# A four-layer convolution chain: eighteen blocks ahead of the projection in layer 0, and waves in pairs in the tail

## The chip, the cores and the metric

The kernel runs on one core of one Trainium2 chip. The metric is the device time of one execution in microseconds (us); what counts is the median over several runs. The core has a matrix engine (TensorE, PE in the profile, with its weight loads as a row of their own, PEld), a vector engine (VectorE, DVE), an engine for activation functions (ScalarE, ACT), a general engine (GpSimd, POOL) and one that here issues the transfers (SyncE, SP). Matmuls write to PSUM, which has eight banks of 128 x 512 float32; DVE and ACT take the results from there to SBUF.

## The reference

The input x is 4 images of 16 channels, 512 x 512, float32. Four layers follow each other.

```python
# layer 0: a window transformer block (windows of 8 x 8, 2 heads of 8, 64 hidden)
x = x + depthwise3x3(x) + pos_b
q, k, v = qkv(affine1(window(x)))
out = softmax(q * 8 ** -0.5 @ k.T) @ v
x = x + (out @ proj_w.T + proj_b)
x = x + gelu(affine2(x) @ fc1_w.T + fc1_b) @ fc2_w.T + fc2_b
# layer 1: fake-quantised 3x3 convolution, batch norm, clip
y = conv(quant(x), quant(weight))
x = clip((y - mean(y)) / sqrt(var(y) + eps) * gamma + beta, 0, 6)
# layer 2: two 3x3 convolutions and a residual
x = conv(relu(conv(x, w1) + b1), w2) + b2 + x
# layer 3: 3x3 convolution, 16 -> 128 -> 16 per pixel, a residual
x = x + (relu(conv(x, conv_w) * w1 + b1) * w2 + b2)
```

The statistics of layer 1 need all of layer 0, and the values of layers 1 to 3 need the statistics. So there are three stretches: layer 0, a pass for the statistics, and a tail that computes layers 1 to 3 together.

## The kernel before

**Layer 0** (`window_attention`) does 64 steps; in each it works on 4 strips pairs by 4 images of a window row. The order of the instructions on every engine is the program's, written out by hand (a manual schedule). A step `n` has two halves. The first runs over eight parts of windows: `scores` (L348) and `values` (L333) on TensorE, the exponential on ACT (L356), `attend` (L369), and on DVE and POOL `divide` (L384, L389, L391) and `turn_back` (L398), which puts the normalised result into `o`. The second half mixes work of three steps on TensorE:

- blocks `q`: queries of step n+1 (L314), emptied to `g` by ACT (L319) in the first part and by DVE (L321) later;
- blocks `d`: one tap of the depthwise convolution of step n+2 for one image (L287), summed in PSUM banks 0 to 3;
- `project` (L404): reads `o`, writes banks 6, 7, 4, 5 in two rounds (one for each head), and DVE adds the result to `y`, one bank at a time (L409);
- blocks `h`: a hidden part of the two-layer perceptron of step n (L416), which reads `y`, each followed by a Gelu on ACT (L421).

One block is four matmuls on one quarter of TensorE's rows; which quarter is given by the block's index modulo 4. Blocks `q` and `h` take PSUM banks 4 to 7 in turn, so each waits until the former user of its bank has been emptied. A string of letters gives the order. Sixteen blocks stand ahead of `project`, 44 behind it:

```python
        for i, what in enumerate("qqddddqqqqdddddd"):
            block(what, i, bank(next(free)) if what == "q" else None, True)
        if more:
            highest(n + 1)
        y = ys.pop(n)
        project(y)
```

Behind the second half come the first `values` and `scores` of the next step, and `output` (L427, L434), which reads the hidden parts.

**The statistics** are a short stretch of bfloat16 convolutions, which the change does not touch.

**The tail** (`conv_layers`) is a software pipeline over 128 tiles of four image rows. In step `T` each stage works on another tile: `load(T + 3)` from HBM (L940), `quantised(T + 2)` (DVE L1010, ACT L1013), and on TensorE `stage_z(T)`, layer 1's convolution in bfloat16; `stage_h(T - 1)` and `stage_x(T - 3)`, layer 2; `stage_y(T - 4)`, layer 3's convolution; four waves `wave(T - 6, k)` (L1197), which widen `y` to 128 channels; and `outputs(T - 7)` (L1217), which narrows them again. All four convolutions are matmuls of the same shape, 64 rows by 32 columns, of L1122, eight side by side. A wave is four matmuls of 32 rows by 128 columns side by side, each to a bank of its own. The output has 128 rows by 32 columns. DVE and ACT share the emptying: L1205 and L1207 for the waves, L1181 and L1182 for `y`, L1170 for `x` (DVE alone), L1159 and L1160 for `h`, L1141, L1142 for `z` and, on DVE, L1143, which caps `z` at 0 and 6; L1223 for the output.

PSUM's eight banks go round: `take(n)` gives the next n, whoever asks. A stage that asks waits until the bank's former user has been emptied. A step takes 26 banks: two for each convolution and the output, four for each wave.

Between stages a tile is also copied to a second buffer shifted by two rows (`shift`, `shift_ends`: L1064, L1067), four transfers each for `qo`, `xo`, `ho` and `zo`. SP issues them and the loads and the store (L1226) one after the other in the program's order. `stage_y(T - 4)` reads `xo`, which `stage_x` of the step before made.

The order on TensorE in the tail is that of the calls in the loop: outputs, wave, y, wave, x, wave, h, z, wave.

Of the kernel before, what the change touches and what calls it, by code (L numbers as in the profile page):

```python
# [29 lines left out]
TP = H // 4  # L30
NH, HD = 2, 8
WS = 8
T = WS * WS
# [110 lines left out]
def window_attention(ctx: ExitStack, tc, xw, x1, hots, m, v, peak):  # L144
# [138 lines left out]
    def depthwise(n, tap, u):  # L283

        dy, dx = divmod(tap, 3)
        for vv in range(V):
            nc.tensor.matmul(  # L287
                bank(u)[quad(vv)], taps[quad(u), tap, :],
                xts[n][quad(u), vv, dy : dy + WS, dx : dx + BW],
                start=tap == 0, stop=tap == 8,  # L290
            )

    def position(n, i):

        if n not in ys:
            ys[n] = px.tile([P, U, N], F32, tag="y", name=f"y{n}", bufs=3)
        for u in (2 * i, 2 * i + 1):
            nc.vector.tensor_scalar(  # L298
                by_window(ys[n][:, u]), by_row(bank(u)), v("pos_b"), None, ALU.add
            )  # L300
# [11 lines left out]
    def query(y, h, vv, b, scalar=False):  # L312
        for u in range(U):
            nc.tensor.matmul(  # L314
                b[quad(u)], wg[h][quad(vv)], y[quad(vv), u, :], start=True, stop=True
            )
        out, src = g[:, vv, :, h, :], b.rearrange("p (j t) -> p j t", t=T)
        if scalar:
            nc.scalar.activation(out, src, AF.Identity, bias=gb[:, h : h + 1])  # L319
        else:  # L320
            nc.vector.tensor_scalar(out, src, gb[:, h : h + 1], None, ALU.add)  # L321
# [6 lines left out]
    def values(k):  # L328

        vv, jl = k // 2, 4 * (k % 2)  # L330
        b, t = bank(4 + 2 * (k % 2)), yts[k % 3]
        for jj in range(4):
            nc.tensor.transpose(  # L333
                b[:, P * jj : P * jj + P],
                y2[:, vv, jl + jj].rearrange("p w t -> p (w t)"), m("ident"),
            )
        src = b.rearrange("p (a w c) -> p a w c", w=2, c=C)
        if 0 < k < 7:
            nc.scalar.copy(t[:, :, 0:3:2], src)
        else:  # L340
            nc.vector.tensor_copy(t[:, :, 0:3:2], src)
# [20 lines left out]
    def attend(e, k):  # L362

        t = yts[k % 3]
        for jj in range(4):
            for u in range(U):
                for w in range(2):
                    half = slice(64 * w, 64 * w + 64)
                    nc.tensor.matmul(  # L369
                        bank(4 + 2 * (k % 2) + w)[quad(u), P * jj : P * jj + P],  # L370
                        t[half, U * jj + u, w : w + 2].rearrange("p d c -> p (d c)"),
                        e[half, u, jj, :],
                        start=True, stop=True,
                    )
# [129 lines left out]
    for n in range(STEPS):  # L504
        more, ahead = n + 1 < STEPS, n + 2 < STEPS
        taken, asked = [0] * U, [0] * V

        def block(what, i, b, scalar=False):
            at = i % 4
            if what == "q" and more:  # L510
                query(ys[n + 1], asked[at], at, b, scalar)
                asked[at] += 1
            elif what == "d" and ahead:
                depthwise(n + 2, taken[at], at)
                taken[at] += 1
                if at % 2 and taken[at - 1 : at + 1] == [9, 9]:
                    position(n + 2, at // 2)

        values(0)
        es, ts = {0: scores(0, n)}, {}  # L520
        if last:

            output(*last)
        for k in range(1, 8):
            es[k] = scores(k, n)
            values(k)
            attend(es[k - 1], k - 1)
            ts[k - 1] = divide(k - 1, n, nc.gpsimd)
            if 1 < k < 7:
                turn_back(ts[k - 2], k - 2)  # L530
            if k == 1:
                send(8 * U)
            if k % 2 and more:
                turn_keys(ys[n + 1], k // 2)
            if k < 5:
                highest_output()
        nc.scalar.preload_act_table_set("gelu_and_others")
        attend(es[7], 7)
        ts[7] = divide(7, n, nc.gpsimd)
        for k in (5, 6, 7):  # L540
            turn_back(ts[k], k)
        free = iter((4, 5, 6, 7, 4, 5))
        for i, what in enumerate("qqddddqqqqdddddd"):
            block(what, i, bank(next(free)) if what == "q" else None, True)
        if more:
            highest(n + 1)
        y = ys.pop(n)
        project(y)
        if n % 2 == 0:
            xo = px.tile([P, U, WS, XW], F32, tag="xo", name=f"xo{n}", bufs=1)  # L550
        if not more:
            flag = bounded()

        hids, units, sent = [[] for _ in range(U)], itertools.cycle((6, 7, 4, 5)), 0
        used = [0] * U
        for i, what in enumerate("ddddhdhddhqqhddhdhddhdhddhddhddhdhddddhhddhh"):
            if what == "h":
                at = i % 4  # L560
                u = used[at]
                used[at] += 1
                if not more and sent < u and len(hids[sent]) == U:
                    output(y, xo, hids[sent], (sent,), (sent,), n)
                    send(8, queues)
                    sent += 1
                hids[u].append(hidden(y, u, at, bank(next(units)), n))
            else:
                block(what, i, bank(next(units)) if what == "q" else None)
        if n + 4 < STEPS:  # L570
            xts[n + 4] = load(n + 4)
        if more:
            nc.scalar.preload_act_table_set("natural_log_exp_and_others")
        last = (y, xo, sum(hids, []), range(U), (5, 4, 6, 7), n)
# [372 lines left out]
def conv_layers(ctx: ExitStack, tc, x1, out, cw, cq, sw, m, v, peak):  # L947
# [29 lines left out]
    ze, zo, he, ho = ring("ze", 4), ring("zo", 3), ring("he", 2), ring("ho", 2)  # L977
# [19 lines left out]
    def inner(t):  # L997
        return t[:, :, 1 : W + 1]
# [137 lines left out]
    def stage_z(n):  # L1136

        if not 0 <= n < TP:
            return
        p, z = convolve(cq, ((qe(n), 0), (qo(n), 1))), inner(ze(n))  # L1140
        nc.scalar.activation(z[:, 0], p[0], AF.Identity, bias=shift_by, scale=scale)  # L1141
        nc.vector.tensor_scalar(z[:, 1], p[1], scale, shift_by, ALU.mult, ALU.add)  # L1142
        nc.vector.tensor_scalar(z, z, ACT_MAX, 0.0, ALU.min, ALU.max)  # L1143
        shift_ends(n, ze, zo)

# [42 lines left out]
    def wave(n, k):  # L1188

        if not 0 <= n < TP:  # L1190
            return []
        units, p = [], take(4)
        for q in range(4):
            w, f = divmod((k + q) % 4, 2)
            par = w ^ (q % 2)
            src = ye(n + (w and not q % 2))
            nc.tensor.matmul(  # L1197
                p[q], w1[_quad(q), 1 - par, :], inner(src)[_quad(q), f, :],
                start=True, stop=True,
            )  # L1200
        for q in range(4):
            w, f = divmod((k + q) % 4, 2)
            hd = ld.tile([P, W], F32, tag="hid", name=f"hid{n}_{k}_{q}", bufs=24)
            if next(count) % 2:
                nc.scalar.activation(hd, p[q], AF.Relu, bias=v("l3_b1"))  # L1205
            else:
                nc.vector.tensor_scalar(hd, p[q], v("l3_b1"), 0.0, ALU.add, ALU.max)  # L1207
            units.append((q // 2, 2 * f + w, w ^ (q % 2), hd))
        return units

    def outputs(n, units):

        if not units:
            return
        p, o, seen = take(2), inner(xe(n)), set()
        for r, c, par, hd in units:
            nc.tensor.matmul(  # L1217
                p[r][_quad(c)], w2[:, par], hd,
                start=(r, c) not in seen, stop=(r, c) in seen,
            )  # L1220
            seen.add((r, c))
        for r in range(2):
            nc.vector.scalar_tensor_tensor(  # L1223
                o[:, r], p[r], v("l3_b2"), o[:, r], ALU.add, ALU.add
            )
        nc.sync.dma_start(out[n], o)  # L1226

    units = []
    for T in range(TP + 7):
        if T + 3 <= TP:  # L1230
            load(T + 3)
        outputs(T - 7, units)
        units = wave(T - 6, 0)
        stage_y(T - 4)
        units += wave(T - 6, 1)
        if T + 2 <= TP:
            quantised(T + 2)
        stage_x(T - 3)
        units += wave(T - 6, 2)
        stage_h(T - 1)  # L1240
        stage_z(T)
        units += wave(T - 6, 3)


def _strips(a):
# [127 lines left out]
```

## Time and profile before

| what | value |
|---|---|
| median of 3 runs | 5648.19 us (5645.71 to 5648.49) |
| profiled execution | 5653.74 us |
| its span | 5651.9 us |
| granted TensorE clock, mean | 0.990 |
| TensorE matmul busy | 5441.0 us (96%) |
| DVE busy | 3826.3 us (68%) |
| ACT busy | 3427.9 us (61%) |
| L287 matmuls (taps) | 18432 records, 603 ns each |
| L404, L409 | projection, and DVE's adds behind it |
| L1197 matmuls (waves) | 4096 records, 639 ns each |
| L1217 matmuls (outputs) | 4096 records, 595 ns each |
| L1207, DVE, one wave part | 1024 of 512 columns, 744 ns each |
| L1205, ACT, one wave part | 1024 of 512 columns, 685 ns each |
| `xo<-xe` transfers | 512 of 128.5 KB, 2.4 us from issue to landing |

The profile is of one execution. Its slices cut the span into 40 equal parts; a digit is the busy share in tenths. A timeline has the start of an instruction (or of several alike that follow each other), how long it took, engine, line, operation, and the tiles it writes and reads; in brackets how long the engine was idle before it, and what ended that. "x8" are eight records: a float32 matmul is two passes and has two. Records of matmuls that run side by side on different parts of the array overlap, so their durations do not add up; the distance between starts does. "issue" as the end of an idle time means that the profile shows no wait.

### The profile page before, as it was taken

The page shows a single profiled execution, that of the slowest core. Times are in us where ns is not written, and L with a number is a line of the kernel's source. Part 1 is how long each engine was busy: PE and PEld are TensorE (multiplying, and loading weights), DVE is VectorE, ACT ScalarE, POOL GpSimd, SP SyncE. Part 2 cuts the span into 40 slices and gives each one's busy share as a digit, 9 for nine tenths or more (in the row PEclk, how much of TensorE's full clock was granted, in tenths as well). Part 3 has the DMA queues.
Part 4 walks back from the last instruction along what each step waited for, and adds up shares of the span by engine and source line. Part 5 has one row for each costly group of instructions (what it writes and reads, how often), then busy time and mean ns, then how long its engine had stood idle before and what let it go on. Part 6 is the DMA issues. An engine that isn't in the chain of part 4 may idle for free. (4 is left out here: it accounts for less than half of the span.)

```text
span 5651.9 us, 268227 instructions
## 1 busy us (share of the span) xinstructions
PE 5441.0 (96%) x120912; PEld 2960.7 (52%) x120912; DVE 3826.3 (68%) x5934; ACT 3427.9 (61%) x4610; POOL 707.4 (13%) x692
## 2 busy tenths in 40 slices
PE   7999999999999999999999666999999999999999
PEld 5777777767677777777776332222222222222222
DVE  4667666666667766666666454667677676777676
ACT  3777777777777777777777453444444444444444
POOL 1111111111111111111111452000000000000000
PEclk9999999999999999999999898999999999999999
DMA  2333333332333333333332797767777767777774
GB/s 79 78 76 77 77 74 80 73 80 66 77 72 82 73 82 73 80 73 80 74 79 41 167 246 178 174 174 178 173 178 173 177 173 176 175 175 175 175 177 107
DMA packets 626192, 677.45 MB, mean 120 GB/s; under 512 B 355856, under 2 KB 485008, under 8 KB 616848
## 3 DMA queue, kind: packets, MB, share of 16 engines
q1 hardware_dynamic: 624240, 658.76, 48.6%
q8 instruction: 953, 15.61, 1.2%
q14 instruction: 199, 1.63, 0.1%
q0 software_dynamic: 512, 1.05, 0.1%
q10 hardware_dynamic: 288, 0.39, 0.0%
HBM read 222.45 MB, written 134.48 MB: 63 GB/s over the span
## 5 line engine op out<-in xcount | busy, mean ns | idle before, releaser
L356 ACT ACTIVATE e<-pair 128x1024 f32<-128x1024 f32 x1024 | 993.0, 1022 | 488.8 <-PE pair L348 488.1
L287 PE MATMUL pair<-x,taps 32*32 32x512 f32 x18432 | 1043.2, 603 | 4.2 <-issue 2.4
L1205 ACT ACTIVATE hid<-tb,vec 128x512 f32<-128x512 f32 x1024 | 647.8, 685 | 630.4 <-PE tb L1197 630.4
L384 DVE STREAM_TRANSPOSE a<-bank 128x512 f32<-128x512 f32 x1024 | 669.7, 692 | 320.2 <-PE bank L369 298.6
L391 POOL TENSOR_TENSOR t<-a,r 128x512 f32<-128x512 f32 x512 | 542.0, 1059 | 2561.3 <-DVE r L389 2561.3
L421 ACT ACTIVATE hid<-bank,f1b 128x512 f32<-128x512 f32 x1024 | 653.5, 687 | 332.7 <-PE bank L416 245.7
L348 PE MATMUL pair<-g,y 32*128 32x128 f32 x16384 | 757.7, 286 | 3.7 <-issue 2.0
L1207 DVE TENSOR_SCALAR hid<-tb,vec 128x512 f32<-128x512 f32 x1024 | 718.2, 744 | 27.1 <-PE tb L1197 26.8
L348 PEld LDWEIGHTS pair<-g,y 32*128 32x128 f32 x16384 | 650.5, 186 | 153.5 <-issue 136.6
L416 PE MATMUL bank<-y,fc_e 32*32 32x512 f32 x8192 | 722.3, 610 | 0.6 <-DVE y L409 0.4
L369 PE MATMUL bank<-e,yt 64*32 64x128 f32 x32768 | 604.1, 274 | 22.4 <-ACT e L356 12.8
L287 PEld LDWEIGHTS pair<-x,taps 32*32 32x32 f32 x18432 | 531.3, 103 | 164.6 <-issue 54.8
L1197 PE MATMUL tb<-ye,mat 32*128 32x512 f32 x4096 | 586.1, 639 | 0.0
L369 PEld LDWEIGHTS bank<-e,yt 64*32 64x32 f32 x32768 | 459.6, 106 | 122.1 <-issue 92.1
L1217 PE MATMUL tb<-hid,mat 128*32 128x512 f32 x4096 | 466.0, 595 | 0.0
L298 DVE TENSOR_SCALAR y<-pair,vec 128x512 f32<-128x512 f32 x256 | 180.3, 747 | 349.8 <-PE pair L287 349.8
L1122 PE MATMUL tb<-zo,cw 64*32 64x512 f32 x3096 | 365.7, 598 | 16.2 <-issue 8.9
L1122 PE MATMUL tb<-xo,cw 64*32 64x512 f32 x3096 | 360.5, 592 | 5.9 <-ACT hid L1205 2.1
L1122 PE MATMUL tb<-ho,cw 64*32 64x512 f32 x3072 | 358.4, 592 | 3.7 <-issue 3.2
L1197 PEld LDWEIGHTS tb<-ye,mat 32*128 32x128 f32 x4096 | 162.8, 183 | 377.5 <-issue 370.4
L1122 PE MATMUL tb<-ze,cw 64*32 64x512 f32 x3072 | 359.9, 598 | 0.0
L1122 PE MATMUL tb<-he,cw 64*32 64x512 f32 x3072 | 358.1, 592 | 0.0
(178 smaller groups left out, 7111.1 us busy)
## 6 DMA issues: line engine op xcount, KB each, us to landing
x<-in_xw_dram SPq DMA_DIRECT2D x64, 1320.0 KB, 5.7
zo<-ze SPq DMA_DIRECT2D x512, 128.5 KB, 2.4
ho<-he SPq DMA_DIRECT2D x512, 128.5 KB, 2.4
xo<-xe SPq DMA_DIRECT2D x512, 128.5 KB, 2.4
y<-y SPq DMA_DIRECT2D x2048, 32.0 KB, 2.7
tx<-x SPq DMA_DIRECT2D x256, 256.0 KB, 4.0
out_dram<-xe SPq DMA_DIRECT2D x128, 512.0 KB, 4.6
x<-xo SPq DMA_DIRECT2D x1008, 64.0 KB, 2.8
```

What stands on the lines that cost most here:

```text
L287: nc.tensor.matmul(bank(u)[quad(vv)], taps[quad(u), tap, :], xts[n][quad(u), vv, dy : dy + WS, dx : dx + BW], start=tap == 0, stop=tap == 8,)
L348: nc.tensor.matmul(bank(u)[:, P * jj : P * jj + P], y2[quad(u), vv, jl + jj].rearrange("p w t -> p (w t)"), g[quad(u), vv, jl + jj].rearra ...
L356: nc.scalar.activation(e[:, 2 * i : 2 * i + 2].rearrange("p u j t -> p u (j t)"), pairs[i], AF.Exp,)
L369: nc.tensor.matmul(bank(4 + 2 * (k % 2) + w)[quad(u), P * jj : P * jj + P], t[half, U * jj + u, w : w + 2].rearrange("p d c -> p (d c)"), ...
L384: nc.vector.transpose(a[:, 512 * w : 512 * w + 512], bank(4 + 2 * (k % 2) + w))
L391: engine.tensor_tensor(t.rearrange("p b w c -> p w b c"), top, r.unsqueeze(3).to_broadcast([P, 2, 16, C]), ALU.mult,)
L416: nc.tensor.matmul(b[quad(k)], fc1[quad(vv), quad(k)], y[quad(vv), u, :], start=True, stop=True,)
L421: nc.scalar.activation(hd, b, AF.Gelu, bias=f1b)
L1122: nc.tensor.matmul(p[r][_quad(2 * f + w)], weights[_half(r), odd, dx, :], src[_half(r), f, dx : dx + W], start=dx == 0, stop=dx == 2,)
L1197: nc.tensor.matmul(p[q], w1[_quad(q), 1 - par, :], inner(src)[_quad(q), f, :], start=True, stop=True,)
L1205: nc.scalar.activation(hd, p[q], AF.Relu, bias=v("l3_b1"))
L1207: nc.vector.tensor_scalar(hd, p[q], v("l3_b1"), 0.0, ALU.add, ALU.max)
```

## The change

In layer 0 two `d` blocks are taken out behind the projection and put ahead of it. The index behind it now starts at 2, so each remaining block keeps its quarter of rows as far as its place in the string is unchanged; among the first ten the quarters of single blocks differ, and the first three hidden blocks are of quarters 2, 0, 1 in place of 0, 2, 1.

In the tail the four waves of a step stand in two pairs: both of the first pair behind `stage_y`, both of the second behind `stage_z`. The capping of `z` and its shift are a function of their own, `capped`, called behind the second pair. `outputs` stands at the end of a step and takes the waves of the same step, so the loop has one pass fewer. On TensorE the order becomes y, wave, wave, x, h, z, wave, wave, outputs. On SP the store now stands ahead of the next step's load.

```diff
         free = iter((4, 5, 6, 7, 4, 5))
-        for i, what in enumerate("qqddddqqqqdddddd"):
+        for i, what in enumerate("qqddddqqqqdddddddd"):
             block(what, i, bank(next(free)) if what == "q" else None, True)
...
-        for i, what in enumerate("ddddhdhddhqqhddhdhddhdhddhddhddhdhddddhhddhh"):
+        for i, what in enumerate("ddddhdhhqqhddhdhddhdhddhddhddhdhddddhhddhh", 2):
...
         nc.vector.tensor_scalar(z[:, 1], p[1], scale, shift_by, ALU.mult, ALU.add)
+
+    def capped(n):
+
+        if not 0 <= n < TP:
+            return
+        z = inner(ze(n))
         nc.vector.tensor_scalar(z, z, ACT_MAX, 0.0, ALU.min, ALU.max)
         shift_ends(n, ze, zo)
...
-    units = []
-    for T in range(TP + 7):
+    for T in range(TP + 6):
         if T + 3 <= TP:
             load(T + 3)
-        outputs(T - 7, units)
-        units = wave(T - 6, 0)
         stage_y(T - 4)
-        units += wave(T - 6, 1)
+        units = wave(T - 6, 0) + wave(T - 6, 1)
         if T + 2 <= TP:
             quantised(T + 2)
         stage_x(T - 3)
-        units += wave(T - 6, 2)
         stage_h(T - 1)
         stage_z(T)
-        units += wave(T - 6, 3)
+        units += wave(T - 6, 2) + wave(T - 6, 3)
+        capped(T)
+        outputs(T - 6, units)
```

## The prediction

> **What bounds the kernel now.** I read the page first: the slices, then the chain. TensorE is busy at a full granted clock almost everywhere, and the chain that ended last lies wholly on TensorE lines of the tail (the slices from the 25th on). So a microsecond counts only if TensorE gets it.
>
> ```profile
> PE   7999999999999999999999666999999999999999
> ...
> PEclk9999999999999999999999898999999999999999
> ...
> PE 38%; SPq 0%; DMA 0%; ACT 0%; issue 0%; DVE 0%; DVEq 0%
> ```
>
> A busy TensorE is not one without gaps, so I went on to the timeline of one tail step. Steps are exact repeats: of the 128 distances between first `y` matmuls, 121 are 16.71 to 16.72 us.
>
> ```profile
> 4503.03 1.14 PE L1197 MATMUL tb<-ye,mat 32*128 32x512 f32 x8
> 4503.19 0.59 ACT L1181 COPY ye<-tb 128x512 f32<-128x512 f32 x1 [1.44 <-PE tb L1122]
> 4503.30 0.69 DVE L1182 COPY ye<-tb 128x512 f32<-128x512 f32 x1 [1.20 <-PE tb L1122]
> ...
> 4510.51 0.40 PE L1122 MATMUL tb<-qe,cq 64*32 64x512 bf16 x4
> ...
> 4511.30 1.14 PE L1197 MATMUL tb<-ye,mat 32*128 32x512 f32 x8
> ...
> 4511.58 0.80 DVE L1142 TENSOR_SCALAR ze<-tb,scale,shift 128x512 f32<-128x512 f32 x1
> ...
> 4512.37 3.64 PE L1217 MATMUL tb<-hid,mat 128*32 128x512 f32 x32
> ```
>
> The reader is to see pitches, not durations. In the same timeline weight loads of a float32 convolution come four to a tile row every 0.43 us; that is one pass. A convolution of `y`, `x` or `h` is 6 passes (2.58), a wave 2 (0.86), an output 8 (3.44), the bfloat16 `z` three half passes (0.64). One step is 3 x 2.58 + 4 x 0.86 + 3.44 + 0.64 = 15.26. The other 1.45 us sits where the tile shape changes: a wave takes 1.07 to the next start (4511.30 to 4512.37), 0.21 more than its passes; going into a wave costs 0.13 to 0.16 (`y` 4500.30 to 4503.03 is 2.73); `h` to `z`, both 64*32, costs 0.02.
>
> In layer 0 I read the stretch in which queries, taps, projection and hidden layer follow each other, 18.7 us of a step of about 47.8.
>
> ```profile
> 2014.49 3.67 ACT L319 ACTIVATE g<-bank,gb 128x512 f32<-128x512 f32 x6 [0.97 <-PE bank L314]
> ...
> 2017.60 0.60 PE L287 MATMUL pair<-x,taps 32*32 32x512 f32 x2
> 2017.64 2.29 PE L404 MATMUL bank<-o,wo 32*32 32x512 f32 x50
> ...
> 2019.78 2.73 DVE L409 SCALAR_TENSOR_TENSOR y<-bank,pb,y 128x512 f32<-128x512 f32 x4 [0.34 <-issue]
> ...
> 2021.72 2.13 ACT L421 ACTIVATE hid<-bank,f1b 128x512 f32<-128x512 f32 x3 [3.56 <-PE bank L416]
> ```
>
> These lines come from the answers by engine, put in order of time. The projection (L404) starts in the very stretch in which the last taps (L287) start: there is no hole in front of it to fill. What follows hangs on it: the adds (L409) at a pitch of 0.66, the first hidden block after the first add, the Gelus.
>
> **Part 1, layer 0: two tap blocks ahead of the projection.** Nothing is added or removed; in 62 of the 64 steps two blocks of taps, on rows 0 to 31 and 32 to 63, go from behind the projection to its front. Each is 4 matmuls of 2 passes on one row quarter, so 0.86 us of that quarter. No DMA, DVE or POOL work moves, and ACT's order stays but for which hidden block comes first.
>
> What they leave is idle time: behind the projection TensorE waits for the adds. Hidden blocks start 0.05 us or so after an add frees their bank (medians: add ends 3.23 and 3.88, hidden 3.32 and 3.94 after the projection's start). The later sixth-and-seventh hidden blocks wait for DVE to empty the second query (7.80, then 7.85). So two blocks fewer there bring nothing forward, and all of it moves with the first add.
>
> What they cost: 16 blocks stand from 2013.36 to about 2017.60, 0.265 each, so two make 0.53. By rows it is more: row quarter 0 has the new block, then its projection, and the first add needs that quarter alone, +0.86. There is one slack: the fourth bank of the projection waits for ACT's sixth query (ends 2018.16), and the first add never comes sooner than 1.30 us after that end; the median of 61 steps is 1.43, the step shown 1.62. So 0.1 to 0.3 of the delay may hide behind ACT in some steps. In the step without any taps in front (the last but one) the first add comes 6.02 us after the first query, at the median 6.53: the taps already stick out. Ends 0.3 and 0.86; I take 0.55, nearest to the row of 16 blocks. Sum 62 x 0.55 = **+34 us** (19 to 53).
>
> **Part 2, tail: two double waves.** Order now: y w x w h z w o w. After: y ww x h z ww o. Shape changes fall from eight to five: into a wave twice (0.16, 0.13), out twice (0.21), and `o` to `y`, which the trace does not have. Its bounds: 0.13 (`o` to wave: 3.57 - 3.44) and 0.21; out of a 32-column shape every row shows 0.13 to 0.16, so 0.13.
>
> The Trainium skill speaks for it and against it on one page, TensorEngine Tiling (Array Packing). Its Key Properties say that a change of tiling mode drains TensorE. At this step's own 1.45/8 = 0.18 a change, three fewer would save 0.54 us, 121 x 0.54 = 65 us. Its section on the PSUM bottleneck says that tiling speeds the matmuls up and not the emptying of PSUM, which may become the limit. This decides here: the eight banks go round, and the second wave of each pair takes the banks of the last two stages, its last two those of the convolution just before it. The trace has that case once, at the end, where `h` and `z` have run out:
>
> ```profile
> 5608.71 2.75 PE L1197 MATMUL tb<-ye,mat 32*128 32x512 f32 x16
> 5608.87 1.41 DVE L1170 SCALAR_TENSOR_TENSOR xe<-tb,vec,ze 128x512 f32<-128x512 f32 x2 [1.40 <-PE tb L1122]
> ...
> 5610.33 0.29 PEld L1197 LDWEIGHTS tb<-ye,mat 32*128 32x128 f32 x2 [0.36 <-DVE xe L1170]
> 5611.39 3.64 PE L1217 MATMUL tb<-hid,mat 128*32 128x512 f32 x32
> ```
>
> The last two matmuls of the pair start at 5610.33, 0.05 after DVE's second eviction, and the next stage 1.06 later. I use both figures.
> - Behind `y`: DVE's copy ends 0.96 after the pair's start (4503.30 + 0.69 - 4503.03), the second wave wants the bank at 0.86: +0.15. The pair takes 0.96 + 0.05 + 1.06 = 2.07.
> - Behind `z`: DVE's part ends 1.87 after `z` starts (4512.38 - 4510.51), so the output starts at 1.87 + 0.05 + 1.06 = 2.98 after `z`, 0.28 later than free banks would allow.
> - Sum from `y` to `y`: 2.73 + 2.07 + 2.60 (`x`) + 2.60 (`h`) + 2.98 + 3.57 = 16.55, against 16.71: -0.16.
>
> The cap of `z` goes behind the four DVE units of the pair. It would end 5.3 us after `z` starts; its transfers stand on SP behind those of `h` and do not need it sooner (before, SP issued them 5.3 to 7.4 after `z`), and `h` reads them one step later. The store moves ahead of the next load on SP; the load is used a step later. Both cost nothing under this cover; a late `zo` would hold `h`.
>
> The quantising moves on its engines: DVE does four units, not two, before `L1010`, so `qe` is ready 1.32 later (four units at 0.66) relative to `y`, and with it SP's four `qo` and four `xo` transfers. The last `xo` lands 14.80 (median; 15.65 at the latest of 80 steps) after `y` starts, so then 16.12 (16.97), and the next `y` wants it at 16.55. About one step in five waits, up to 0.4: +0.04 on the mean. So -0.12 a step, 121 x 0.12 = **-14 us** (-19 to -4). In the last steps without `x` four waves stand together where three did: +2. One pass of the loop fewer saves nothing; the same matmuls run.
>
> **Sum.** +34 - 14 + 2 = +22 on the profiled execution's 5653.74 (span 5651.9). That execution lies 5.5 above the median of the runs, 5648.19; moved onto the median: **5670 us**.
>
> **Rivals.**
> - *ACT hides the taps.* If the first add hangs on ACT's sixth query in most steps, the two blocks cost nothing: 5648 - 12 = 5636. For it: the correlation of the add with that query's end, 0.78. Against: 0.13 to 0.32 us lie between them already. Faster by 0.2%, on the other side.
> - *The waves pay in full.* If the banks come free in time, the skill's 65 us count: 5648 + 34 - 65 = 5617. Against: the stall at 5610.33.
> - *The transfers decide.* If `xo` lands 0.5 later on average than I move it, every `y` waits about 0.4 more, from the point where landing passes 16.55: 121 x 0.3 = +36 in place of -14: 5648 + 34 + 36 + 2 = 5720. For it: SP issues back to back from `qo` to the store.
> - *The taps move nothing* because the planner restores the order: excluded, the program's order shows them in front.
>
> **Chances.** My forecast 0.60, ACT hides 0.19, full pay 0.08, transfers 0.13. No change means within 11 us, about what a measurement here can tell. The forecast's own range is 5650 to 5697 and reaches into no change with a small part. Slower 0.64, same 0.16, faster 0.20. The range for 8 in 10: 5630 to 5703.
>
> **What would show it.** Right: the first L409 add 0.4 to 0.9 later after the first query, layer 0 steps near 48.4; tail steps 16.5 to 16.65, weight loads of the second wave released by DVE `ye` and `ze`. Wrong: the add unmoved (ACT hides), steps near 16.2 (full pay), or `y` waiting for `xo` in most steps.

## The result, and the profile after

| | before | after |
|---|---|---|
| median of 4 runs each | 5646.95 us (5642.49 to 5648.49) | 5702.02 us (5687.94 to 5703.92) |
| ratio, 95% interval | | 1.0096 (1.0076 to 1.0117) |
| profiled execution, its span | 5653.74, 5651.9 us | 5700.55, 5698.7 us |
| granted clock, mean | 0.990 | 0.992 |
| layer 0: start to the first matmul of the last projection | 3118.3 us | 3176.2 us |
| from there to the first `y` matmul | 385.5 us | 383.0 us |
| tail: first `y` matmul to the end | 2148.1 us | 2139.6 us |
| one step of layer 0, mean of steps 3 to 60 | 47.83 us | 48.86 us |
| one steady tail step, mean of 121 | 16.715 us | 16.605 us |

The kernel became slower by 55 us where +22 was forecast. The three stretches of the profiled executions add up to the spans' difference: +57.8 - 2.5 - 8.5 = +46.8. So all of the loss is in layer 0, and the tail gained.

First the page of after: two rows of slices, and the Gelu group (partitions x elements, count | busy us, ns of one | idle us of ACT ahead of the group, and what ended most of it).

```profile
PE   7999999999999999999999765999999999999999
...
PEclk9999999999999999999999998999999999999999
...
L421 ACT ACTIVATE hid<-bank,f1b 128x512 f32<-128x512 f32 x1024 | 638.6, 686 | 402.2 <-PE bank L416 378.8
```

The same group on the page of before:

```profile
L421 ACT ACTIVATE hid<-bank,f1b 128x512 f32<-128x512 f32 x1024 | 653.5, 687 | 332.7 <-PE bank L416 245.7
```

Slices and clock read as before: they cannot show a per cent. The Gelu group can. It does the same 1024 activations at the same 686 ns, but ACT's idle time ahead of them grew by 69.5 us, and it ends with TensorE's hidden matmuls (L416). Something in front of the hidden layer is late.

The timeline of one layer 0 step of after, with the lines of three engines put in order of time, shows where:

```profile
2058.00 0.66 PE L314 MATMUL bank<-y,wg 32*32 32x512 f32 x8
...
2059.13 3.67 ACT L319 ACTIVATE g<-bank,gb 128x512 f32<-128x512 f32 x6 [1.19 <-PE bank L314]
...
2062.68 0.61 PE L404 MATMUL bank<-o,wo 32*32 32x512 f32 x1
...
2065.39 2.73 DVE L409 SCALAR_TENSOR_TENSOR y<-bank,pb,y 128x512 f32<-128x512 f32 x4 [1.39 <-issue]
...
2067.64 1.84 ACT L421 ACTIVATE hid<-bank,f1b 128x512 f32<-128x512 f32 x3 [4.85 <-PE bank L416]
```

Counted from the first query (2058.00; in the step shown of before 2013.36), the first add stands at 7.39 where it stood at 6.42, and the first Gelu at 9.64 where it stood at 8.36. ACT's queries are no later (2059.13 is 1.13 after the first query, as 2014.49 was). The distance from the add to the Gelu grew as well, from 1.94 to 2.25, although nothing there was touched but the order of the hidden blocks. Means over the steps, in us from the first query:

| | before | after |
|---|---|---|
| first projection matmul | 4.20 | 5.02 |
| end of ACT's sixth query | 5.21 | 5.13 |
| first add | 6.67 | 7.38 |
| first hidden matmul | 7.55 | 8.49 |
| first Gelu | 8.69 | 9.78 |
| last Gelu's end | 20.35 | 21.25 |
| the whole step | 47.83 | 48.86 |

The waits of ACT between 1000 and 3000 us say it once more (us in total, times, longest). Before:

```profile
ACT hid L421 <- PE bank L416: 147.5, 129, 3.9
ACT hid L421 <- DVE y L409: 51.8, 15, 3.8
```

After:

```profile
ACT hid L421 <- PE bank L416: 241.2, 155, 5.1
...
ACT hid L421 <- DVE y L409: 4.0, 1, 4.0
```

Per step that is 199.3 / 41.8 = 4.8 us before and 245.2 / 40.9 = 6.0 after.

The timeline of one tail step of after, TensorE with two lines of DVE (wave lines are L1203 now, outputs L1223):

```profile
4588.55 2.14 PE L1203 MATMUL tb<-ye,mat 32*128 32x512 f32 x16
...
4588.82 0.69 DVE L1188 COPY ye<-tb 128x512 f32<-128x512 f32 x1 [1.45 <-PE tb L1122]
...
4590.61 0.63 PE L1122 MATMUL tb<-he,cw 64*32 64x512 f32 x4
...
4595.79 0.39 PE L1122 MATMUL tb<-qe,cq 64*32 64x512 bf16 x4
...
4596.60 2.24 PE L1203 MATMUL tb<-ye,mat 32*128 32x512 f32 x16
...
4596.86 0.80 DVE L1142 TENSOR_SCALAR ze<-tb,scale,shift 128x512 f32<-128x512 f32 x1
...
4597.53 0.47 PEld L1203 LDWEIGHTS tb<-ye,mat 32*128 32x128 f32 x6 [0.20 <-ACT ze L1141]
...
4598.77 3.64 PE L1223 MATMUL tb<-hid,mat 128*32 128x512 f32 x32
...
4602.34 0.63 PE L1122 MATMUL tb<-xo,cw 64*32 64x512 f32 x4
```

The pair behind `y` takes 4590.61 - 4588.55 = 2.06, the output starts 4598.77 - 4595.79 = 2.98 after `z`, and the output takes 4602.34 - 4598.77 = 3.57 to the next `y`. Weight loads of the second pair wait for the eviction of `z` (4597.53). In the pair behind `y` the profile records no such wait. But of its second wave's four matmuls the last, which writes the bank that DVE empties, starts at 4589.56, 0.05 after DVE's copy ends (4588.82 + 0.69), and its second pass comes at 4590.10, where the other three have theirs at 4589.95. The step from 4585.81 to 4602.34 is 16.53.

### The profile page after: what moved, and what is told of

It is laid out like the page before. It is cut to its first block, busy times and chain, and to the rows that moved or that the text cites. A ratio compares the mean times of both kernels' runs of the same rounds, so it can differ in the third digit from the quotient of the medians.

```text
span 5698.7 us, 268595 instructions
## 1 busy us (share of the span) xinstructions
PE 5485.7 (96%) x120912; PEld 3116.7 (55%) x120912; DVE 3826.3 (67%) x5934; ACT 3386.4 (59%) x4610; POOL 707.5 (12%) x692
## 5 line engine op out<-in xcount | busy, mean ns | idle before, releaser
L287 PE MATMUL pair<-x,taps 32*32 32x512 f32 x18432 | 1022.3, 601 | 2.9 <-DVE y L298 1.5
L421 ACT ACTIVATE hid<-bank,f1b 128x512 f32<-128x512 f32 x1024 | 638.6, 686 | 402.2 <-PE bank L416 378.8
L1213 DVE TENSOR_SCALAR hid<-tb,vec 128x512 f32<-128x512 f32 x1024 | 697.7, 745 | 39.8 <-PE tb L1203 27.3
L416 PE MATMUL bank<-y,fc_e 32*32 32x512 f32 x8192 | 696.2, 600 | 0.8 <-DVE y L409 0.6
L1211 ACT ACTIVATE hid<-tb,vec 128x512 f32<-128x512 f32 x1024 | 619.6, 688 | 112.1 <-PE tb L1203 111.8
L287 PEld LDWEIGHTS pair<-x,taps 32*32 32x32 f32 x18432 | 504.1, 103 | 186.1 <-issue 66.1
L1203 PE MATMUL tb<-ye,mat 32*128 32x512 f32 x4096 | 564.6, 622 | 0.0
L1187 ACT COPY ye<-tb 128x512 f32<-128x512 f32 x129 | 75.7, 587 | 659.5 <-PE tb L1122 659.5
L1223 PE MATMUL tb<-hid,mat 128*32 128x512 f32 x4096 | 466.0, 595 | 0.0
L1203 PEld LDWEIGHTS tb<-ye,mat 32*128 32x128 f32 x4096 | 256.1, 183 | 261.6 <-issue 219.7
```

Of the source, the lines that this page charges most:

```text
L287: nc.tensor.matmul(bank(u)[quad(vv)], taps[quad(u), tap, :], xts[n][quad(u), vv, dy : dy + WS, dx : dx + BW], start=tap == 0, stop=tap == 8,)
L416: nc.tensor.matmul(b[quad(k)], fc1[quad(vv), quad(k)], y[quad(vv), u, :], start=True, stop=True,)
L421: nc.scalar.activation(hd, b, AF.Gelu, bias=f1b)
L1203: nc.tensor.matmul(p[q], w1[_quad(q), 1 - par, :], inner(src)[_quad(q), f, :], start=True, stop=True,)
L1223: nc.tensor.matmul(p[r][_quad(c)], w2[:, par], hd, start=(r, c) not in seen, stop=(r, c) in seen,)
```

## The experiments

Each run was timed against the kernel before on the same chip. Layer 0 of the five kernels that have the order of before there differs between profiles (steps of 47.78, 47.83, 47.94, 48.00 and 48.01 us, mean 47.91), so a difference of 0.2 in a step means little alone. The changed kernel's step is 1.03 over before's own profile and 0.95 over that mean. Steadier is the stretch inside a step from the first add to the last Gelu's end: 13.67 or 13.68 us in all five. Such marks are read beside the step. Tails are compared by their own steps.

### The two halves of the change apart

`l0_alone` is the kernel before with the two strings of layer 0 from the change:

```
-        for i, what in enumerate("qqddddqqqqdddddd"):
+        for i, what in enumerate("qqddddqqqqdddddddd"):
...
-        for i, what in enumerate("ddddhdhddhqqhddhdhddhdhddhddhddhdhddddhhddhh"):
+        for i, what in enumerate("ddddhdhhqqhddhdhddhdhddhddhddhdhddddhhddhh", 2):
```

> Layer 0 as changed, the tail as before. The changed kernel's layer 0 took 47.83 to 48.86 us a step, some 58 us over all its steps. If the two parts do not touch each other, this run is 55 to 62 us over before. If the two parts share something (the same loads, the clock), it differs from 58 by more than 10.

`tail_alone` is the changed kernel with the two strings of before.

> The tail as changed, layer 0 as before. By the sum of the tail (16.72 to 16.61 a step over 121 steps, 4 to 5 us more at both ends): 7 to 12 us under before. If the double waves paid what three changes of shape cost, it would be 65 under; if they only cost, it is over before.

| | median, before beside it | ratio (95%) | layer 0 step | tail step |
|---|---|---|---|---|
| `l0_alone` | 5710.02, 5645.74 | 1.0109 (1.0091 to 1.0126) | 48.92 | 16.715 |
| `tail_alone` | 5632.5, 5645.74 | 0.9976 (0.9966 to 0.9985) | 47.78 | 16.612 |

The halves do not touch each other: their ratios multiply to 1.0085, inside the interval of the whole, and each has the step lengths of the changed kernel. Layer 0 costs about 64 us alone (51 to 71 by the interval, 55 to 62 expected), the tail brings 13 (9 to 19, 7 to 12 expected).

### Which quarters the two blocks load

The blocks of the change lie on row quarters 0 and 1. Both of these kernels keep the order of the hidden blocks of before (quarters 0, 2, 1) and take two blocks to the front, on quarters 0 and 1 or on 2 and 3. `rows_0_1`:

```
-        for i, what in enumerate("qqddddqqqqdddddd"):
+        for i, what in [*enumerate("qqddddqqqqdddddd"), (0, "d"), (1, "d")]:
...
         for i, what in enumerate("ddddhdhddhqqhddhdhddhdhddhddhddhdhddddhhddhh"):
+            if i in (0, 1):
+                continue
```

> Two tap blocks ahead of the projection as in the change, on row quarters 0 and 1, but the order behind it is that of before with these two left out, so the hidden blocks keep their quarters 0, 2, 1. Theory of the row quarter (a new block holds up the projection of its own quarter, 0.86 us, and the first add needs quarter 0): first add +0.7 to +0.86 a step, 43 to 55 us. Theory of the queue (each block ahead costs 0.265 us of TensorE wherever it is): +0.53, 33 us. Theory of ACT (the add hangs on ACT's last query): 0. What this run is under the run of layer 0 alone is the price of the order of the hidden blocks.

`rows_2_3` has 2 and 3 in place of 0 and 1 in both places.

> The same with the two blocks on row quarters 2 and 3. Theory of the row quarter: quarters 2 and 3 are needed by the third and fourth add, 1.3 and 2.0 us after the first, so the first add moves only as far as the in-order issue of the projection's fourth part holds up its fifth: 0.1 to 0.5 a step, 6 to 31 us, and clearly less than on quarters 0 and 1. Theory of the queue: the same 33 us as on quarters 0 and 1. Theory of ACT: 0.

| us from the first query | before | `rows_0_1` | `rows_2_3` | `l0_alone` |
|---|---|---|---|---|
| first projection matmul | 4.20 | 5.04 | 4.87 | 5.02 |
| first add | 6.67 | 7.43 | 7.31 | 7.39 |
| first hidden matmul | 7.55 | 8.24 | 8.11 | 8.49 |
| first Gelu | 8.69 | 9.37 | 9.24 | 9.79 |
| step | 47.83 | 48.57 | 48.37 | 48.92 |

`rows_0_1` took 5682.48 against 5645.74, ratio 1.006 (1.0036 to 1.0083); `rows_2_3` 5671.59, 1.0056 (1.0039 to 1.0072).

Three things follow. First, with blocks on quarters 2 and 3, quarter 0, which the first add needs, has no new work, and still its projection starts 0.67 later and the add 0.64, where 0.1 to 0.5 was expected if only the row quarter counted. The projection stands behind the two blocks in TensorE's order and pays for them wherever they lie. Second, on quarters 0 and 1 the projection starts 0.84 later, near the quarter's 0.86, and the add 0.76: lying on the add's own quarter costs 0.17 more at the projection and 0.12 at the add. Over the mean of five, the step is 0.66 longer on quarters 0 and 1, and 0.46 on 2 and 3. By time the two cannot be told apart: 37 us (20 to 47) and 26 us (22 to 41) over before, with 33 expected from the queue in both, and 43 to 55 and 6 to 31 from the row quarter. So the queue counts, and ACT, from which 0 was expected in both, does not. That the quarter adds to it is likely, but small beside the noise: the five kernels of one order differ by up to 0.13 at the projection and 0.09 at the add. Third, `rows_0_1` has the same adds as `l0_alone` to 0.04, and its hidden matmuls 0.25 and its Gelus 0.42 earlier. These two differ only behind the projection: `rows_0_1` has two taps and then the hidden block of quarter 0, `l0_alone` four taps and then that of quarter 2.

From the timeline of `rows_2_3`, the first four blocks of a step, its adds and its first Gelus:

```profile
2036.48 0.66 PE L314 MATMUL bank<-y,wg 32*32 32x512 f32 x8
2036.53 0.69 PE L287 MATMUL pair<-x,taps 32*32 32x512 f32 x8
...
2043.70 2.73 DVE L409 SCALAR_TENSOR_TENSOR y<-bank,pb,y 128x512 f32<-128x512 f32 x4 [1.22 <-issue]
...
2045.63 2.00 ACT L421 ACTIVATE hid<-bank,f1b 128x512 f32<-128x512 f32 x3 [4.09 <-PE bank L416]
```

From add to Gelu it is 1.93, as before (1.94), not 2.25. The first two lines show that the forecast's 0.265 is the mean of a full queue and not the price of a place in it: two query blocks and two taps, on four different quarters, all start here within 0.13 us. Once every quarter has work, a block can start only when its own quarter is free, and the program's order keeps what stands behind it waiting; that this is how blocks on quarters 2 and 3 hold up quarter 0 is read from the order, not shown by a run of its own.

### The order of the hidden blocks alone

`hidden_2_first` leaves the front of before as it is and only lets the hidden block of quarter 2 come ahead of that of quarter 0, as the change does:

```
-        for i, what in enumerate("ddddhdhddhqqhddhdhddhdhddhddhddhdhddddhhddhh"):
+        for i, what in [
+            (0, "d"), (1, "d"), (2, "d"), (3, "d"), (2, "h"), (1, "d"), (0, "h"),
+            *[*enumerate("ddddhdhddhqqhddhdhddhdhddhddhddhdhddddhhddhh")][7:],
+        ]:
```

> The kernel before, with the first two hidden blocks exchanged, so that the one on row quarter 2 stands first; number and place of all tap blocks as before, first add unmoved. If the order of the hidden blocks is what the changed layer 0 paid beyond the two blocks (its step was 0.35 us over that of rows_0_1), because quarter 2 is still busy with its part of the projection and a tap when the first add is done: first Gelu 0.2 to 0.45 later, 12 to 28 us over before. If the 0.35 came from how the taps fall behind the projection, this run is the same as before.

It took 5669.99 against 5651.67, ratio 1.0029 (1.0019 to 1.0038), with a layer 0 step of 48.23 (+0.40, and 0.32 over the mean of five). The medians are 18 us apart, where 12 to 28 was expected; over 63 steps that is 0.29 a step. The same two lines of its timeline, and between them the first weights and the first matmuls of the hidden layer:

```profile
2038.57 2.73 DVE L409 SCALAR_TENSOR_TENSOR y<-bank,pb,y 128x512 f32<-128x512 f32 x4 [0.28 <-issue]
...
2039.43 0.10 PEld L416 LDWEIGHTS bank<-y,fc_e 32*32 32x32 f32 x1
...
2039.86 0.64 PE L416 MATMUL bank<-y,fc_e 32*32 32x512 f32 x4
...
2040.96 1.84 ACT L421 ACTIVATE hid<-bank,f1b 128x512 f32<-128x512 f32 x3 [3.97 <-PE bank L416]
```

The same place in before:

```profile
2020.59 0.13 PEld L416 LDWEIGHTS bank<-y,fc_e 32*32 32x32 f32 x5
2020.59 0.62 PE L416 MATMUL bank<-y,fc_e 32*32 32x512 f32 x2
```

The add is where it was (mean 6.67 in both), and the Gelu follows 2.39 later, not 1.94; means of the first hidden matmul and the first Gelu are +0.36 and +0.39. No tap was moved ahead of the projection here. So swapping two hidden blocks, which the forecast costed at nothing, takes time.

The trace shows where the time goes. The weights of the first hidden block are loaded 0.21 us after the add's end (0.12 in before), so the wait for the add is over. Yet its matmul starts another 0.41 later (median of 57 steps), nearly a pass of 0.43. In before, `rows_0_1` and `rows_2_3`, where quarter 0 comes first, that distance is 0.00; in after and `l0_alone`, where quarter 2 does, it is 0.41 and 0.40. So the block waits for work that is still on the array. That this is the work of its own quarter is read from the program's order: the first add needs the projection of quarter 0 alone, which stands first in each half of it. When that add is done, quarter 0 is through with its projection, while quarter 2's share stands two places later in each half; each of them has one tap between its projection and its hidden block.

Half of the delay is made up again before the hidden layer ends: from the first add to the last Gelu's end it is 13.87 where the five kernels have 13.67 or 13.68. So 0.19 of the step's growth is sure, and the rest lies behind the last Gelu, where profiles of one order differ by 0.15. The order of the hidden blocks costs 0.2 to 0.3 us a step.

### Fourteen blocks ahead

If sixteen is too few or eighteen too many, fourteen should tell which way the optimum lies.

```
-        for i, what in enumerate("qqddddqqqqdddddd"):
+        for i, what in [*enumerate("qqddddqqqqdd"), (2, "d"), (3, "d")]:
...
-        for i, what in enumerate("ddddhdhddhqqhddhdhddhdhddhddhddhdhddddhhddhh"):
+        for i, what in [(0, "d"), (1, "d"), *enumerate("ddddhdhddhqqhddhdhddhdhddhddhddhdhddddhhddhh")]:
```

> Layer 0 with two tap blocks (quarters 0 and 1) taken from ahead of the projection to behind it: fourteen in front. If a block ahead costs its 0.27 us both ways until ACT's sixth query decides (the first add is 0.13 over that bound at the median): 0.1 to 0.3 a step less, 6 to 18 us under before. If the idle time behind the projection is too small to take four more blocks' worth of taps, no gain or slower.

The gain did not come, the second case did: 5694.24 against 5651.67, ratio 1.0071 (1.0053 to 1.009). Its timeline:

```profile
2050.32 2.73 DVE L409 SCALAR_TENSOR_TENSOR y<-bank,pb,y 128x512 f32<-128x512 f32 x4 [0.45 <-issue]
...
2053.26 1.84 ACT L421 ACTIVATE hid<-bank,f1b 128x512 f32<-128x512 f32 x3 [4.25 <-PE bank L416]
```

The add did come forward (mean 6.48, -0.19), a good part less than the 0.53 of two blocks, since with less in front ACT's sixth query (5.16) holds it: in 57 of 61 steps the add comes 1.30 to 1.35 after that query's end, in before in 17. But the two blocks now stand behind the projection, ahead of the hidden block, and from add to Gelu it is 2.94. Means: first hidden matmul 8.11 (+0.56), first Gelu 9.42 (+0.73), step 48.58 (+0.75). So of the three numbers tried sixteen is the best, with a cost on either side: more in front delays the projection, more behind delays the hidden block.

### The waits for `xo` in the tail

In the waits of TensorE's weight loads of after, between 3750 and 5500 us (about 105 steps), stand one for the eviction of `z` and one for `xo`, as the forecast had them (the one for `ye` that it named as well is not among them):

```profile
PEld tb L1203 <- ACT ze L1141: 21.7, 105, 0.2
PEld tb L1122 <- DMA xo<-xe: 12.9, 20, 0.9
```

The second pair waits for `z`'s eviction in every step, `y` for `xo` in 20 of 105. `tail_x_first` moves the shifts of the quantised input behind the convolution that reads `h`, so that they do not stand on SP ahead of the `xo` transfers. On `tail_alone`:

```
         if T + 2 <= TP:
-            quantised(T + 2)
+            scaled(T + 2)
+            rounded(T + 2)
         stage_x(T - 3)
+        if T + 2 <= TP:
+            shift(T + 2, qe, qo, T + 2 < TP)
```

> The tail as changed, layer 0 as before, but SP issues the shift of x ahead of that of q. If the steps above 16.53 us (30 of 121, mean 0.087) come from xo landing after y wants it, they go: mean 16.53, some 10 us under the run of the tail alone, 23 under before. If they come from something else, they stay.

Its waits in the same stretch have no line for `xo` or `ho` any more, keep that for `z` (21.7 us in 105 steps), and have a small one for `qo`:

```profile
PEld tb L1122 <- DMA qo<-qe: 2.5, 3, 0.8
```

Yet it gained nothing, where 23 us under before were expected: 5650.13 against 5651.67, ratio 0.9994 (0.9981 to 1.0008), and its tail steps are 16.632 on the mean (`tail_alone` 16.612) with a median of 16.613 where `tail_alone` has 16.525. Its tail is 2145.8 us long, 3.4 more than that of `tail_alone`; what else parts the two medians lies ahead of the tail, where the programs are the same. The waits went as expected; in their place almost every step (119 of 121) is about 0.09 longer. The first four matmuls of the `ho` half of a convolution in `tail_x_first`, and then in `tail_alone`:

```profile
4507.37 0.75 PE L1122 MATMUL tb<-ho,cw 64*32 64x512 f32 x4
```

```profile
4510.07 0.63 PE L1122 MATMUL tb<-ho,cw 64*32 64x512 f32 x4
```

The four take 0.12 longer because three of the tiles start 0.12 later than the first. The convolutions behind, which have the same shape, carry that offset until the shape changes: `z` to the wave takes 0.93, not 0.81. Between the first tile and the other three the trace of `tail_x_first` has a semaphore instruction of its own on TensorE (0.05 us, in 103 of 105 steps), behind which the next weight load starts 0.09 later. `tail_alone` has none there in 105 steps, and no offset. The two kernels of the next section repeat this: the one with the moved shifts has both the instruction and the offset, the one without has neither. So the moved shifts cost a wait instruction more at this place, and with it comes the offset.

### `z` ahead of `h`

If the second pair stalls because `z` was just written to the banks that it wants, then letting the longer convolution `h` come last takes part of the stall away. `z_ahead` is `tail_alone` with that swap alone, `tail_z_h` is `tail_x_first` with it:

```
-        stage_h(T - 1)
         stage_z(T)
+        stage_h(T - 1)
```

> As tail_x_first, and z ahead of h on TensorE, so that the convolution in front of the second pair of waves is h, whose emptying on DVE is shorter (0.75 for 0.80) and does not queue behind another's. If the bank of the convolution just before a pair is what holds up its second wave: the stall of 0.28 shrinks to about 0.2, the step to 16.45, some 9 us under tail_x_first. If the stall is due to the change of shape alone, no difference.

> The tail as changed with z ahead of h as its one further edit; layer 0 and the order of the shifts as before. Bank theory, as in tail_z_h: the step without any wait falls from 16.525 to 16.45. In tail_x_first the waits for xo went, but the three convolutions in a row came out 0.12 longer, with one DMA wait more in TensorE's program. If that was the price of the extra wait, it is absent here, and the waits for xo are back: mean 16.53 to 16.56, with some 30 steps above the rest, 14 to 18 us under before in time. If z ahead of h costs by its later h (ho lands later for x), steps wait for ho and the mean is above 16.6.

| | median, before beside it | ratio (95%) | tail step, mean | shortest | over the shortest by 0.05 |
|---|---|---|---|---|---|
| `tail_alone` | 5632.5, 5645.74 | 0.9976 (0.9966 to 0.9985) | 16.612 | 16.521 | 30 of 121 |
| `tail_x_first` | 5650.13, 5651.67 | 0.9994 (0.9981 to 1.0008) | 16.632 | 16.525 | 119 of 121 |
| `tail_z_h` | 5637.08, 5651.67 | 0.9972 (0.9956 to 0.9988) | 16.556 | 16.454 | 120 of 121 |
| `z_ahead` | 5637.81, 5650.41 | 0.9975 (0.9965 to 0.9984) | 16.548 | 16.452 | 37 of 121 |

In both the shortest step fell by 0.07, to the 16.45 expected from the bank; from the change of shape alone no difference was expected. `tail_z_h` has the offset of `tail_x_first` in nearly every step again, `z_ahead` has it not. The mean of `z_ahead` is the one expected (16.53 to 16.56); its time is 13 us under before, where 14 to 18 was expected. The waits of `z_ahead`:

```profile
PEld tb L1122 <- DMA xo<-xe: 20.3, 29, 0.9
...
PEld tb L1203 <- ACT he L1165: 1.7, 11, 0.2
```

The wait of the second pair for an eviction fell from 21.7 us in 105 steps to 1.7 in 11, and a shorter step waits for `xo` more often (29 times, not 20). The swap is worth 0.06 x 121 = 8 us in the tail's own length (2134.9 from 2142.4), which the whole-kernel medians cannot tell apart: `tail_alone`, `z_ahead` and `tail_z_h` are all faster than before by a quarter of a per cent, and none is shown to be the best. All three keep layer 0 as it was.

## Why the prediction was right in sign and short in size

**The tail: right, by its steps.** The sum gave 16.55 without waits; measured 16.53, with the pair behind `y` 2.06 (2.07 in the sum), the output 2.98 after `z` (2.98), and 3.57 from output to `y` (3.57). The last `xo` lands 16.31 after `y` starts (median of the 20 of 80 steps for which the trace has that landing; 16.12 in the sum, whose 14.80 rested on 30 such steps and not on 80). `qe` is 1.32 later as reckoned, and SP issues the last `xo` 1.44 later. So 20 of 105 steps wait, about the one in five named. The steady steps give 121 x 0.110 = -13.3 us for the -14, and the last steps cost +2.0 for the +2. The three first steps took 46.5 us where before's profile has 43.7. That is not the change's: the five other profiles with the tail of before have 46.9 to 48.8 there. So the tail's gain is nearer to 11 us than to the 8.5 of the two profiles.

**The rule on mode changes and the one on PSUM both count.** Above its passes (15.26) the new step has 1.27 us. Taken apart: into a wave 0.16 and 0.17, out of waves 0.34 and 0.45, out of outputs 0.13, between like shapes 0.02. If leaving a wave still takes the 0.21 that it took before, 0.13 and 0.24 of these are the banks' stalls. Then the changes of shape fell from 1.43 to about 0.88, nearly the 0.54 that the forecast worked out from this trace's 0.18 a change and from the rule in the Trainium skill's TensorEngine Tiling (Array Packing), Key Properties, that a change of tiling mode drains TensorE. The emptying of PSUM took about 0.4 of it back. Full pay, the rival at 5617, fell on the banks, as the forecast said. For the pair behind `z` the run `z_ahead` bears this out; for the pair behind `y` no run varied it.

**Layer 0: the failed term is "62 x 0.55 = +34".** Measured, layer 0 alone costs 64 us, and a step is 0.95 to 1.03 longer (over the mean of five, over before's own profile). Over the mean of five the 0.95 divides into three: the first add comes 0.72 later, from it to the last Gelu's end it is 0.19 more (13.87), and the rest of the step has 0.03. Two parts of the term were off:

- *The two blocks themselves: right in kind, somewhat small.* The sum took the row of sixteen blocks, 0.53, with a slack behind ACT and the row quarter's 0.86 as ends. Apart from the order of the hidden blocks the two cost 0.66 a step on the quarters that the change uses, and 0.46 on quarters 2 and 3. The first add moved by 0.71, inside the 0.4 to 0.9 named. ACT hid nothing: its sixth query's end stands still (5.21, 5.13), the median distance from it to the add went from 1.43 to 2.29, and no step of after has less than 1.85. That is the end of the rival at 5636. The correlation that spoke for it (0.78 in the forecast; over 61 steps the trace gives 0.96) decides nothing, since the add follows the projection's first matmul just as closely (0.95).
- *"ACT's order stays but for which hidden block comes first", costed at nothing.* This is what was missed. By itself it is worth 18 us (`hidden_2_first`), 0.2 to 0.3 a step; from `rows_0_1` to `l0_alone`, where two taps ahead of the hidden block come with it, the step grows by 0.35, of which 0.18 lies between first add and last Gelu. The forecast looked at when a bank is freed and not at when the quarter that the block runs on is.

Together 0.66 and 0.3 make the 0.95. That the two blocks taken away behind bring nothing forward was right: in `rows_2_3` first add to last Gelu's end is 13.67 us where before had 13.68.

**The range.** The sign came from the mechanism that the forecast gave: the taps ahead of the projection cost more than the waves in pairs bring. But 5702 is above the forecast's own range, 5650 to 5697, and inside the one for 8 in 10 by a single microsecond; nothing in the sum led there, so that it is inside is luck.

**The transfers as the bound, 5720,** did not come: waits for `xo` stay at 12.9 us in 105 steps. The time came near that rival's through layer 0, not through it.

## What to carry to other kernels

When a block is moved ahead in a common queue, price what waits behind it there as well as the part of the array that it uses, and then read the order of everything behind it again: which hidden block comes first was worth 0.2 to 0.3 us a step, beside the 0.5 to 0.7 of the two blocks. Fewer changes of matmul shape pay only if the banks that the bunched stages want are empty by then; work out each bank's last eviction before counting the changes. A change with two halves is measured in halves: here one was worth keeping and the other hid it.

## What was not expected of the hardware

- Small matmuls run side by side on different row quarters, and four blocks on four quarters start within 0.13 us. Still two blocks on quarters 2 and 3 delayed work on quarter 0, which had nothing new ahead of it there, by 0.67 us (`rows_2_3`, the projection).
- Putting one hidden block ahead of another, on a row quarter whose projection was issued later, delayed the first Gelu by 0.39 us with the add where it was (`hidden_2_first`), its weights being loaded 0.41 us before its matmul started; two more taps ahead of the hidden block delayed it by 0.73 although the add came 0.19 earlier (`fourteen`).
- A wait instruction more on TensorE made three of four tiles start 0.12 us late in one convolution (`tail_x_first`), and that was still there three convolutions on, and was paid for at the next change of shape. A wait that comes and goes in 20 of 105 steps cost less than an offset in all.
